# Order of data sums, bias joining and row transfers in a fused attention and non-local block

## The chip, the cores and the metric

One core of a Trainium2 chip runs the whole program. The metric is the device time in microseconds (us) of one execution; lower is better. The engines that matter are TensorE (PE in the profile: matrix products; PEld is its weight load), VectorE (DVE), ScalarE (ACT), GpSimd (POOL) and SyncE (SP), which issues the transfers (DMA).

## The reference

Eight images of 512 channels and 32 x 32 points, all in float32. Each goes through two layers:

```
# layer 0: attention, 8 heads of 64 channels
q, k, v = Wq x + bq,  Wk x + bk,  Wv x + bv          # 1x1 convolutions
out = softmax(q^T k / 8) v                            # per head, 1024 x 1024
x = x + Wp out + bp
# layer 1: non-local block, 256 inner channels
theta, phi, g = Wtheta x + bt,  Wphi x + bp2,  Wg x + bg
z = W ((theta phi^T / 1024) g) + bW + x
# then, per channel, over all images and points:
out = (z - mean(z)) / sqrt(var(z) + 1e-5) * gamma + beta
```

## The kernel before

The eight images are worked one after the other; the loop over `b` is unrolled, so the program is one long stream on each engine. An image passes through the stages attention (scores `ps`, weighted values `po`), q of the next image (`pq`), denominators (`den`), v of the next image (`pv`), k of the next image (`pk`), projection (`pp`), theta and phi (`ptp`), g (`pg`), theta times phi (`pf`), and the second layer's output (`pz`). Image 6 puts off its g and z, so that attention of image 7 follows its theta and phi at once.

**Seven products for eight.** Each 1x1 convolution is a product of 2 x 2 blocks done by a Strassen-Winograd scheme (`seven`, from L232): seven block products instead of eight, at the price of sums. The data sums are made by `data_sums` (L185): from the quarters 11, 12, 21, 22 of the data, t1 = 12 - 11, t2 = 22 - t1, t3 = 22 - 12, t4 = 21 - t2, each of 128 x 1024 on VectorE. The products use them in the order 11, t1, t2, 22, t3, 21, t4. In q, k and (images 1 to 6) the projection, two of the seven are split once more: `nested` (L217) runs small products between the large ones, on the inner sums of 21 and of t4 (`inner_sums`, four operations of 128 x 256 each). A product's result stands in a pair of PSUM banks; `first` takes it out with a bias, `add` adds it to another quarter. The next product that writes the bank waits until that is done. Four such pairs (`s0` to `s3`) rotate: the list `free` gives their order, and `next_bank` takes the next one.

**The order on an engine.** A scheduler orders each engine's instructions by priority, which is program order, and by when it reckons that their inputs are ready. Those given to `pe`, `dve` or `sp` (one function, `keep_in_program_order`) keep their order among themselves. On the chip each engine then takes its instructions in that fixed order. Blocks of 128 x 1024 (`block`) come from a ring of ten, shared by the exponentials, the data sums and other helpers; a new one waits for a block that is no longer read.

**Around the change.**
- End of attention: two steps before its end `near_end` makes the four data sums of the next image. The last exponential is summed into `acc` (L424). The last weighted values leave PSUM by a copy on ScalarE (L444) and a sum on VectorE (L445); the bank that they leave is one of the two that q's nested products take. Then come the inner sums of 21.
- `normalize` (L479) brings the reciprocals of the softmax denominators, one row per head and half, to all partitions: for each half h, group g of four units and head j of a pair, one transfer of 64 partitions x 2 rows of 2 KB into `r`. The transfers are issued before v; the four products `o * r` (L493) come after the fifth of v's seven products (`{4: normalize(d)}`). The data sums of o follow during k (`sums_of_o`).
- `bound_scores` (L375) multiplies the peaks of q and k, sums them over a head on TensorE (`bound`), compares (`gates`, L381) and multiplies q by the gate on GpSimd (L383), four operations of 128 x 1024. For images 1 to 7 it runs after the fifth product of the projection; for image 0 in v.
- `theta_phi` (L526): the result of the first product leaves PSUM by one sum on VectorE (L536), which frees the bank for the third product. Its data sums are all made before.
- `join_bias` (L173), once, ahead of the projection of image 0: Wp bv is added to bp, by 16 products with a single column, each of two passes, hence 32 matmuls in the profile.

Of the kernel before, what the change touches and what calls it, by code (L numbers as in the profile page):

```python
# [30 lines left out]
def unshifted(ctx: ExitStack, tc: tile.TileContext, a: dict, out: bass.AP):  # L31
# [31 lines left out]
    def pe(ins):  # L63
        tc.keep_in_program_order(ins)
# [8 lines left out]
    def next_bank(name):  # L73
        free.append(free.pop(0))
        return bank(free[-1], name)
# [96 lines left out]

    def join_bias(w):  # L173

        ps = next_bank("pbp")[:, 0, :CC]
        for oc in range(CC):
            m, mc = divmod(oc, CC // 2)
            for c in range(CC):
                k, kc = divmod(c, CC // 2)
                quarter = {(0, 0): w[:, 0], (0, 1): w[:, 1], (1, 0): corner["WpT"], (1, 1): w[:, 2]}[m, k]  # L180
                pe(nc.tensor.matmul(ps[:, oc:oc + 1], quarter[:, kc, mc * P:(mc + 1) * P], bv[:, c:c + 1],
                                    start=(c == 0), stop=(c == CC - 1), skip_group_check=True))
        nc.vector.tensor_tensor(bp, bp, ps, ALU.add)

    def data_sums(quarters, name, width=2, pin=lambda ins: None, midway=lambda: None):  # L185

        b11, b12, b21, b22 = quarters
        t = [block(f"t{i}_{name}")[:, :width, :] for i in range(4)]
        pin(nc.vector.tensor_tensor(t[0], b12, b11, ALU.subtract))  # L189
        pin(nc.vector.tensor_tensor(t[1], b22, t[0], ALU.subtract))  # L190
        midway()
        pin(nc.vector.tensor_tensor(t[2], b22, b12, ALU.subtract))
        pin(nc.vector.tensor_tensor(t[3], b21, t[1], ALU.subtract))
        return {"11": b11, "21": b21, "22": b22, "t1": t[0], "t2": t[1], "t3": t[2], "t4": t[3], "name": name}

    def inner_sums(data, which):
# [4 lines left out]
        nc.vector.tensor_tensor(t[:, 0], b12, b11, ALU.subtract)  # L201
        nc.vector.tensor_tensor(t[:, 1], b22, t[:, 0], ALU.subtract)
        nc.vector.tensor_tensor(t[:, 2], b22, b12, ALU.subtract)
        nc.vector.tensor_tensor(t[:, 3], b21, t[:, 1], ALU.subtract)
# [157 lines left out]
    def values(b, w, data, between=None):  # L362
        v = mats.tile([P, NB, C], F32, tag="v", name=f"v_{b}")

        def at(q):
            return v[:, (int(q[1]) - 1) * NB // 2:int(q[1]) * NB // 2, (int(q[0]) - 1) * C // 2:int(q[0]) * C // 2]

        def as_v(ps):
            return ps.rearrange("p h (i f) -> p (h i) f", f=C // 2)

        seven(f"pv_{b}", w, data, True, lambda q, ps: nc.scalar.copy(at(q), as_v(ps)),  # L371
              lambda q, ps: nc.vector.tensor_tensor(at(q), at(q), as_v(ps), ALU.add), between)
        return v

    def bound_scores(b, q, k, peak_q, peak_k):  # L375
# [14 lines left out]
    def attention(b, q, k, v, near_end, make_f=None):  # L390
# [16 lines left out]
        def scores(i):  # L407
            u, m = steps[i]
            p, h = units[u]
            ps = bank(tags[(0, 1, 3)[i] if i < 3 else (i + 1) % 2], f"ps_{b}_{u}_{m}")  # L410
            for j in range(2):
                r = slice(j * D, (j + 1) * D)
                for c in range(2):
                    keys = slice(m * P + c * P // 2, m * P + (c + 1) * P // 2)
                    pe(nc.tensor.matmul(ps[c * P // 2:(c + 1) * P // 2, j, :], k[r, p, keys],  # L415
                                        q[r, p, h * 512:(h + 1) * 512], start=True, stop=True, skip_group_check=True))
            e = block(f"e_{b}_{u}_{m}")
            nc.scalar.activation(e, ps, AF.Exp, scale=SCALE)  # L418
            es[u, m] = e
            if m == 1:  # L420
                accs[u] = w3.tile([P, 2, 512], F32, tag="acc", name=f"acc_{b}_{u}")
                nc.vector.tensor_tensor(accs[u], es[u, 0], e, ALU.add)  # L422
            elif m > 1:
                nc.vector.tensor_tensor(accs[u], accs[u], e, ALU.add)  # L424
            if m == NB - 1 and u == len(units) - 1 and make_f:
                near_end(lambda: spread(u, dve))
            elif m == NB - 1:
                spread(u)

        def weighted(i):  # L430
            u, m = steps[i]
            p, _ = units[u]
            if m == 0:
                sums[u] = bank(tags[2 + u % 2], f"po_{b}_{u}")
            ps, e = sums[u], es.pop((u, m))
            for r in range(2):
                keys = slice(r * P // 2, (r + 1) * P // 2)
                for j in range(2):
                    pe(nc.tensor.matmul(ps[j * D:(j + 1) * D, r, :], v[keys, m, (2 * p + j) * D:(2 * p + j + 1) * D],  # L439
                                        e[keys, j, :], start=(m == 0), stop=(m == NB - 1), skip_group_check=True))  # L440
            if m == NB - 1:
                if not o:
                    o["o"] = mats.tile([P, CC, N], F32, tag="o", name=f"o_{b}")
                nc.scalar.copy(part(u), ps[:, 0, :])  # L444
                nc.vector.tensor_tensor(part(u), part(u), ps[:, 1, :], ALU.add)  # L445

        def spread(u, pin=lambda ins: None):

# [30 lines left out]
        def normalize(d):  # L479

            r = foldp.tile([P, 8, 512], F32, tag="fold", name=f"r_{b}")
            for h in range(NH):
                for g in range(2):
                    for j in range(2):
                        rows_of = d[g].rearrange("(j p h s) n -> j h s p n", j=2, p=2, h=NH)[j, h, 0]
                        sp(nc.sync.dma_start(r[j * D:(j + 1) * D, 4 * g + h:4 * g + 4:2, :],
                                             rows_of.partition_broadcast(D)))

            def products():
                for h in range(NH):  # L490
                    for g in range(2):
                        at = o["o"][:, 2 * g:2 * g + 2, h * 512:(h + 1) * 512]
                        dve(nc.vector.tensor_tensor(at, at, r[:, 4 * g + h:4 * g + 4:2, :], ALU.mult))  # L493

            return products
# [27 lines left out]
              early=b == B - 1, inner="WpT" if 0 < b < B - 1 else None)  # L523


    def theta_phi(b, w, data):  # L526
        tp = mats.tile([P, NB, 2 * CI], F32, tag="o", name=f"tp_{b}")

        def at(q):
            return tp[:, (int(q[1]) - 1) * NB // 2:int(q[1]) * NB // 2, (int(q[0]) - 1) * CI:int(q[0]) * CI]  # L530

        def as_tp(ps):
            return ps.rearrange("p h (i f) -> p (h i) f", f=CI)

        seven(f"ptp_{b}", w, data, True,
              lambda q, ps: nc.vector.tensor_tensor(  # L536
                  at(q), as_tp(ps), tpb[:, int(q[0]) - 1].to_broadcast([P, NB // 2, CI]), ALU.add),
              lambda q, ps: nc.vector.tensor_tensor(at(q), at(q), as_tp(ps), ALU.add))
        return tp

    def make_f(b, tp, ps):
# [183 lines left out]
    for b in range(B):  # L725
# [5 lines left out]
        def near_end(midway=None):  # L731
            if last:
                nxt["data"] = data_sums(quarters_of(held["x"]), f"x1_{b - 1}_again", pin=dve, midway=midway)
            else:
                nxt["data"] = data_sums(quarters_of(nxt["x"]), f"x_{b + 1}")

        def held_f(ps):
            held["f"] = make_f(b - 1, held["tp"], ps)
# [288 lines left out]
```

## Time and profile before

| | |
|---|---|
| three timed executions | 2188.3, 2189.35, 2190.09 us |
| the profiled execution | 2190.26 us, span in the profile 2188.5 us |
| mean granted TensorE clock | 0.994 |
| one attention | 110 us |
| from one attention to the next, images 1 and 2 | 267.3 us |
| the same, image 3 | 272.1 us |

The profile is that of one execution. A timeline line reads: start, duration (both us), engine, source line, operation, output<-inputs, shape, count, and in brackets the idle time ahead of it with what ended it. A waits line reads: engine and line that waited, what for, us in total, times, longest. Matmuls of float32 run in two passes, so one product is two entries. A matmul's recorded end is modelled and overlaps the next one's start, so the distance between starts tells more than the duration.

### The profile page before, as it was taken

What the parts mean: (1) busy time and instruction counts of PE and PEld (TensorE: products, weight loads), DVE (VectorE), ACT (ScalarE), POOL (GpSimd) and SP (SyncE); (2) the same over time, 40 slices, a digit from 0 to 9 for tenths busy, and PEclk for the clock granted to TensorE, in tenths of its full rate; (3) what the DMA queues carried; (4) which work ended last, traced back from release to release, by engine and by line L of the source; (5) the groups of instructions that cost most, each with busy time, mean ns of one, the idle gap of its engine ahead of it and who ended that gap; (6) DMA issues with size and microseconds to landing.
All of it is one profiled execution on the core that took longest, in us unless ns stands there. A gap on an engine that the chain in (4) does not pass through costs nothing.

```text
span 2188.5 us, 29703 instructions
## 1 busy us (share of the span) xinstructions
PE 2149.1 (98%) x12478; PEld 1113.0 (51%) x12478; DVE 1434.5 (66%) x1612; ACT 741.6 (34%) x848; POOL 52.5 (2%) x36
## 2 busy tenths in 40 slices
PE   9999999999999999999999999999999999999996
PEld 4534664346633467335573356633666336643362
DVE  6477656777567764777647777477773677657736
ACT  1463103641046310463104631056212652056115
POOL 0000000000100001000010000100000000100000
PEclk9999999999999999999999999999999999999998
DMA  6312433114131231312413123231234114121559
GB/s 214 133 39 58 129 149 120 40 39 154 68 130 40 65 118 67 131 40 73 111 68 130 40 77 107 100 108 40 87 134 160 40 40 130 51 63 41 185 209 358
DMA packets 59405, 223.41 MB, mean 102 GB/s; under 512 B 9856, under 2 KB 16256, under 8 KB 53760
## 3 DMA queue, kind: packets, MB, share of 16 engines
q1 hardware_dynamic: 57776, 220.12, 31.1%
q8 instruction: 100, 1.64, 0.3%
q10 hardware_dynamic: 1488, 1.32, 0.2%
q14 instruction: 41, 0.34, 0.0%
HBM read 138.03 MB, written 49.81 MB: 86 GB/s over the span
## 4 chain that ended last, share of the span: by engine, by line
PE 87%; DVE 8%; DMA 2%; issue 1%; ACT 1%; SPq 0%; DVEq 0%
PE ps L415 20%; PE po L439 19%; PE ptp L268 7%; PE pp L268 7%; PE pv L268 7%; PE pk L268 6%; PE pq L268 5%; PE pg L268 4%; PE pf L546 3%; PE pz L268 2%; PE pk_in_s L231 2%; PE pq_in_s L231 2%; PE pp_in_s L231 2%; PE pz L656 2%; PE pwf L581 1%
## 5 line engine op out<-in xcount | busy, mean ns | idle before, releaser
L418 ACT ACTIVATE e<-ps 128x1024 f32<-128x1024 f32 x512 | 522.9, 1025 | 428.9 <-PE ps L415 424.0
L424 DVE TENSOR_TENSOR acc<-acc,e 128x1024 f32<-128x1024 f32 x384 | 470.1, 1224 | 129.4 <-ACT e L418 122.0
L439 PE MATMUL po<-e,v 64*64 64x512 f32 x4096 | 528.7, 589 | 0.7 <-ACT w_WgT L548 0.7
L415 PE MATMUL ps<-q,k 64*64 64x512 f32 x4096 | 529.1, 589 | 0.0
L439 PEld LDWEIGHTS po<-e,v 64*64 64x64 f32 x4096 | 156.5, 133 | 283.4 <-issue 275.4
L415 PEld LDWEIGHTS ps<-q,k 64*64 64x64 f32 x4096 | 155.6, 133 | 284.1 <-issue 274.7
L569 ACT ACTIVATE g<-pg,gb 128x512 f32<-128x512 f32 x31 | 21.3, 687 | 399.1 <-PE pg L268 396.2
L422 DVE TENSOR_TENSOR acc<-e,e 128x1024 f32<-128x1024 f32 x64 | 78.2, 1222 | 108.7 <-ACT e L418 73.4
L268 PE MATMUL ptp<-w_tp,t_x 128*128 128x256 f32 x512 | 116.3, 380 | 5.2 <-DVE tp L536 5.2
L268 PE MATMUL pv<-w_WvT,t_x 128*128 128x256 f32 x512 | 114.5, 379 | 0.0
L268 PEld LDWEIGHTS ptp<-w_tp,t_x 128*128 128x128 f32 x512 | 96.7, 190 | 20.9 <-DVE tp L536 8.1
L268 PEld LDWEIGHTS pv<-w_WvT,t_x 128*128 128x128 f32 x512 | 97.2, 190 | 13.2
L268 PE MATMUL pp<-t_o,w_WpT 128*128 128x512 f32 x208 | 101.0, 593 | 0.5 <-DVE t_o L189 0.5
L268 PE MATMUL pk<-t_x,w_WkT 128*128 128x512 f32 x200 | 100.1, 598 | 0.0
L268 PE MATMUL pq<-t_x,w_WqT 128*128 128x512 f32 x200 | 98.8, 593 | 0.3 <-DVE w_WqT L708 0.3
L371 ACT COPY v<-pv 128x1024 f32<-128x1024 f32 x32 | 32.4, 1012 | 191.2 <-PE pv L268 191.2
L383 POOL TENSOR_SCALAR q<-q,gates 128x1024 f32<-128x1024 f32 x32 | 52.2, 1649 | 1848.2 <-DVE gates L381 1848.2
L268 PE MATMUL ptp<-w_tp,x 128*128 128x256 f32 x384 | 87.4, 381 | 0.2 <-DVE x L290 0.2
L268 PE MATMUL pv<-w_WvT,x 128*128 128x256 f32 x384 | 87.5, 381 | 0.0
L268 PEld LDWEIGHTS pv<-w_WvT,x 128*128 128x128 f32 x384 | 72.4, 190 | 15.7 <-issue 5.9
L268 PEld LDWEIGHTS ptp<-w_tp,x 128*128 128x128 f32 x384 | 72.4, 190 | 11.0 <-DVE x L290 1.0
L466 DVE TENSOR_TENSOR fold<-fold 128x1024 f32<-128x1024 f32 x48 | 58.7, 1222 | 26.1 <-DMA fold<-acc 25.6
(186 smaller groups left out, 2216.0 us busy)
## 6 DMA issues: line engine op xcount, KB each, us to landing
fold<-acc SPq DMA_DIRECT2D x254, 128.0 KB, 2.3
r<-den_d SPq DMA_DIRECT2D x64, 256.0 KB, 7.0
x<-in_x_dram SPq DMA_DIRECT2D x31, 512.0 KB, 6.1
w_WqT<-kept_WqT SPq DMA_DIRECT2D x7, 2176.0 KB, 8.7
w_WkT<-kept_WkT SPq DMA_DIRECT2D x7, 2176.0 KB, 8.4
w_WpT<-kept_WpT SPq DMA_DIRECT2D x6, 2176.0 KB, 8.8
w_WvT<-kept_WvT SPq DMA_DIRECT2D x7, 1792.0 KB, 7.1
w_tp<-kept_tp SPq DMA_DIRECT2D x7, 1792.0 KB, 7.3
```

The source lines that it names most:

```text
L231: pe(nc.tensor.matmul(ps, a[wi], d[di], start=s not in begun, stop=True, skip_group_check=True))
L268: pe(nc.tensor.matmul(to_ps, lhsT(k), rhs(k), start=(s, at) not in begun, stop=(k == nk - 1), skip_group_check=True))
L371: seven(f"pv_{b}", w, data, True, lambda q, ps: nc.scalar.copy(at(q), as_v(ps)), lambda q, ps: nc.vector.tensor_tensor(at(q), at(q), as_v( ...
L383: nc.gpsimd.tensor_scalar(q[:, p, :], q[:, p, :], gate[:, p:p + 1], 1.0, ALU.mult, ALU.mult)
L415: pe(nc.tensor.matmul(ps[c * P // 2:(c + 1) * P // 2, j, :], k[r, p, keys], q[r, p, h * 512:(h + 1) * 512], start=True, stop=True, skip_gr ...
L418: nc.scalar.activation(e, ps, AF.Exp, scale=SCALE)
L422: nc.vector.tensor_tensor(accs[u], es[u, 0], e, ALU.add)
L424: nc.vector.tensor_tensor(accs[u], accs[u], e, ALU.add)
L439: pe(nc.tensor.matmul(ps[j * D:(j + 1) * D, r, :], v[keys, m, (2 * p + j) * D:(2 * p + j + 1) * D], e[keys, j, :], start=(m == 0), stop=(m ...
L466: return [lambda to=to, l=l, r=r: pin(nc.vector.tensor_tensor(to, l, r, ALU.add)) for to, l, r in ((t[:, 0], t[:, 0], t[:, 1]), (t[:, 2], ...
L546: pe(nc.tensor.matmul(ps[:, c, :], tp[:, i, c * P:(c + 1) * P], tp[:, i, CI:], start=(i == 0), stop=(i == NB - 1)))
L656: pe(nc.tensor.matmul(ps[:, h - h0, :], wf[:, d, oc * P:(oc + 1) * P], g[d][:, h * 512:(h + 1) * 512], start=(d == 0), stop=(d == IC - 1), ...
```

## The change

Five things:

1. `data_sums` can make some of the four sums, and `more_sums` the rest later. For the next image's q, t1 and t2 stay near the end of attention; t3 and t4 follow after the inner sums of 21. All of these from the last `acc` and last `o` sum on are held in program order, the inner sums of t4 too. For theta/phi, t1 and t2 stay ahead; t3 and t4 come after the sum that takes out the first product.
2. `bound_scores` moves from the projection to theta/phi, after its fourth product.
3. `normalize` brings the rows by four transfers of four rows each instead of eight of two; the products `o * r` come after v's sixth product instead of its fifth.
4. The sums into v are held in program order.
5. `join_bias` multiplies the blocks of Wp by bv and sums them over the four chunks on GpSimd (eight scalings and six sums of 128 x 256), into a block of the ring; TensorE then needs four products with a column of ones.

```diff
     def join_bias(w):
+        t = block("wp_bv")
+        half = C // 2
+        for m, quarters in enumerate(((w[:, 0], w[:, 1]), (corner["WpT"], w[:, 2]))):
+            to, one = (t[:, i, m * half:(m + 1) * half] for i in range(2))
+            for c in range(CC):
+                nc.gpsimd.tensor_scalar(one if c else to, quarters[c // 2][:, c % 2, :], bv[:, c:c + 1], 1.0,
+                                        ALU.mult, ALU.mult)
+                if c:
+                    nc.gpsimd.tensor_tensor(to, to, one, ALU.add)
         ps = next_bank("pbp")[:, 0, :CC]
         for oc in range(CC):
-            m, mc = divmod(oc, CC // 2)
-            for c in range(CC):
...
+            pe(nc.tensor.matmul(ps[:, oc:oc + 1], t[:, 0, oc * P:(oc + 1) * P], ones, start=True, stop=True,
+                                skip_group_check=True))
         nc.vector.tensor_tensor(bp, bp, ps, ALU.add)
...
+    def data_sums(quarters, name, which=(1, 2, 3, 4), **how):
+        data = dict(zip(("11", "12", "21", "22"), quarters), name=name)
+        more_sums(data, which, **how)
+        return data
+
+    def more_sums(data, which, pin=lambda ins: None, midway=lambda: None):
+        for i in which:
+            l, r = {1: ("12", "11"), 2: ("22", "t1"), 3: ("22", "12"), 4: ("21", "t2")}[i]
+            if i == 3:
+                midway()
+            data[f"t{i}"] = block(f"t{i}_{data['name']}")
+            pin(nc.vector.tensor_tensor(data[f"t{i}"], data[l], data[r], ALU.subtract))
...
         seven(f"pv_{b}", w, data, True, lambda q, ps: nc.scalar.copy(at(q), as_v(ps)),
-              lambda q, ps: nc.vector.tensor_tensor(at(q), at(q), as_v(ps), ALU.add), between)
+              lambda q, ps: dve(nc.vector.tensor_tensor(at(q), at(q), as_v(ps), ALU.add)), between)
...
-                nc.vector.tensor_tensor(accs[u], accs[u], e, ALU.add)
+                ins = nc.vector.tensor_tensor(accs[u], accs[u], e, ALU.add)
+                if i == len(steps) - 1 and not make_f:
+                    dve(ins)
...
-                nc.vector.tensor_tensor(part(u), part(u), ps[:, 1, :], ALU.add)
+                ins = nc.vector.tensor_tensor(part(u), part(u), ps[:, 1, :], ALU.add)
+                if i == len(steps) - 1 and not make_f:
+                    dve(ins)
...
-            for h in range(NH):
-                for g in range(2):
-                    for j in range(2):
-                        rows_of = d[g].rearrange("(j p h s) n -> j h s p n", j=2, p=2, h=NH)[j, h, 0]
-                        sp(nc.sync.dma_start(r[j * D:(j + 1) * D, 4 * g + h:4 * g + 4:2, :],
-                                             rows_of.partition_broadcast(D)))
+            for g in range(2):
+                for j in range(2):
+                    rows_of = d[g].rearrange("(j i s) n -> j s i n", j=2, i=4)[j, 0]
+                    sp(nc.sync.dma_start(r[j * D:(j + 1) * D, 4 * g:4 * g + 4, :], rows_of.partition_broadcast(D)))
...
-    def theta_phi(b, w, data):
+    def theta_phi(b, w, data, between):
...
+        def first(q, ps):
+            ins = nc.vector.tensor_tensor(at(q), as_tp(ps), tpb[:, int(q[0]) - 1].to_broadcast([P, NB // 2, CI]),
+                                          ALU.add)
+            if q == "11":
+                dve(ins)
+
+        seven(f"ptp_{b}", w, data, True, first,
+              lambda q, ps: nc.vector.tensor_tensor(at(q), at(q), as_tp(ps), ALU.add),
+              {0: lambda: more_sums(data, (3, 4), pin=dve), **between})
...
-                nxt["data"] = data_sums(quarters_of(nxt["x"]), f"x_{b + 1}")
+                nxt["data"] = data_sums(quarters_of(nxt["x"]), f"x_{b + 1}", (1, 2))
...
-            inner_sums(nxt["data"], "21")
+            inner_sums(nxt["data"], "21", dve)
+            more_sums(nxt["data"], (3, 4), dve)
             q, peak_q = heads_of(b + 1, "q", weights("WqT"), bq, nxt["data"], dve, inner="WqT",
-                                 between={1: lambda: inner_sums(nxt["data"], "t4")}, fills=last_fold)
+                                 between={1: lambda: inner_sums(nxt["data"], "t4", dve)}, fills=last_fold)
             load_w(nc.sync)
             d = [denominators(g, next_bank(f"den_{b}_{g}")[:, 0, :]) for g in range(2)]
-            v = values(b + 1, weights("WvT"), nxt["data"], {4: normalize(d)})
+            v = values(b + 1, weights("WvT"), nxt["data"], {5: normalize(d)})
...
-            between = {4: lambda: bound_scores(b + 1, q, k, peak_q, peak_k)}
...
-        data = data_sums(quarters_of(xt), f"x1_{b}")
+        data = data_sums(quarters_of(xt), f"x1_{b}", (1, 2))
...
-        tp = theta_phi(b, weights("tp"), data)
+        tp = theta_phi(b, weights("tp"), data, {} if last else {3: lambda: bound_scores(b + 1, q, k, peak_q, peak_k)})
```

More of the change, by code (lines that the diff above doesn't have):

```diff
@@ L175, in join_bias @@
         ps = next_bank("pbp")[:, 0, :CC]
         for oc in range(CC):
-            m, mc = divmod(oc, CC // 2)
-            for c in range(CC):
[L179 to L182, printed above, removed]
@@ L183, in join_bias @@
-        nc.vector.tensor_tensor(bp, bp, ps, ALU.add)
[L185 to L194, printed above, removed]
@@ L196, in inner_sums @@
-    def inner_sums(data, which):
+            pe(nc.tensor.matmul(ps[:, oc:oc + 1], t[:, 0, oc * P:(oc + 1) * P], ones, start=True, stop=True,
+                                skip_group_check=True))
+        nc.vector.tensor_tensor(bp, bp, ps, ALU.add)
+    def data_sums(quarters, name, which=(1, 2, 3, 4), **how):
[9 more added lines that the diff above has]
+            pin(nc.vector.tensor_tensor(data[f"t{i}"], data[l], data[r], ALU.subtract))
@@ L198, in inner_sums @@
+    def inner_sums(data, which, pin=lambda ins: None):
         d, name = data[which], f"{which}_{data['name']}"
@@ L200, in inner_sums @@
         t = block(f"i_{name}").rearrange("p a (b n) -> p (a b) n", b=2)
[L201 to L204, printed above, removed]
+        pin(nc.vector.tensor_tensor(t[:, 0], b12, b11, ALU.subtract))
+        pin(nc.vector.tensor_tensor(t[:, 1], b22, t[:, 0], ALU.subtract))
+        pin(nc.vector.tensor_tensor(t[:, 2], b22, b12, ALU.subtract))
+        pin(nc.vector.tensor_tensor(t[:, 3], b21, t[:, 1], ALU.subtract))
         data[f"inner {which}"] = {"11": b11, "21": b21, "22": b22, **{f"t{i + 1}": t[:, i] for i in range(4)}}
@@ L533, in as_tp @@
             return ps.rearrange("p h (i f) -> p (h i) f", f=CI)
[L535 to L538, printed above, removed]
+        def first(q, ps):
[6 more added lines that the diff above has]
+              {0: lambda: more_sums(data, (3, 4), pin=dve), **between})
         return tp
```

## The prediction

> **What bounds the kernel now.** I read the busy shares first, then TensorE's own waits, then the timeline of each place those waits name. The busy shares say that TensorE is the bound:
>
> ```profile
> PE 2149.1 (98%) x12478; PEld 1113.0 (51%) x12478; DVE 1434.5 (66%) x1612; ACT 741.6 (34%) x848; POOL 52.5 (2%) x36
> ```
>
> So a gain can come only from gaps in TensorE's stream or from matmuls left out. Its waits, the longest groups:
>
> ```profile
> PE ptp L268 <- DVE tp L536: 5.2, 7, 0.8
> PE pq_in_s L231 <- DVE o L445: 5.0, 7, 0.7
> PE pk_in_s L231 <- DVE k L290: 3.2, 2, 2.8
> ```
>
> Two come once in each of the images 0 to 6; the third comes in two images only. Busy time runs on past a matmul's start, so I price a wait by starts. The wait in q, image 0, on TensorE and VectorE:
>
> ```profile
> 193.69 1.02 PE L268 MATMUL pq<-t_x,w_WqT 128*128 128x512 f32 x2
> 195.42 0.70 PE L231 MATMUL pq_in_s<-i_x,w_WqT 128*128 128x256 f32 x2 [0.71 <-DVE o L445]
> 195.96 1.02 PE L268 MATMUL pq<-t_x,w_WqT 128*128 128x512 f32 x2
> 194.69 0.68 DVE L445 TENSOR_TENSOR o<-o,po 128x512 f32<-128x512 f32 x1
> ```
>
> The pair at 193.69 takes 0.86 (the step before, 192.40 to 193.26), so the next was due at 194.55 and came 0.87 late; it then took 0.54 to the next start where its kind takes 0.43. **Price 0.97 us.** VectorE's sum frees the bank that the nested product writes; it stood behind four sums of data and eight inner ones. The wait in theta/phi, image 1:
>
> ```profile
> 569.98 3.72 PE L268 MATMUL ptp<-w_tp,t_x 128*128 128x256 f32 x16 [0.76 <-DVE tp L536]
> 566.74 2.06 DVE L193 TENSOR_TENSOR t_x<-x,t_x 128x1024 f32<-128x1024 f32 x1
> 568.72 2.34 DVE L536 TENSOR_TENSOR tp<-ptp,tpb 128x1024 f32<-128x1024 f32 x2
> ```
>
> The product before began at 565.61 and takes 3.45, so 569.06 was due: 0.92 late, 0.10 more in its own run (573.54 follows after 3.56). **Price 1.02 us**, 0.93 in image 0. Third, join_bias in image 0:
>
> ```profile
> 266.78 0.99 PE L181 MATMUL pbp<-bvc,w_WpT 128*128 128x1 f32 x4
> 267.64 6.15 PE L268 MATMUL pp<-o,w_WpT 128*128 128x512 f32 x8
> 267.60:273.60 6.00, 6.00 (x9) 2.58 (x10) 2.41 (x3) 0.00 (x0) 0.00 (x0) 0.58 0.01 3
> ```
>
> The last is a stretch with its granted clock, 0.58. The 32 passes of one column run from 263.26 to 267.64, and the eight passes of the projection after them take 5.98 where such eight take 3.43 elsewhere. Fourth, the k stage, which normalize feeds, in images 1 and 3:
>
> ```profile
> 517.28 1.23 DVE L493 TENSOR_TENSOR o<-o,r 128x1024 f32<-128x1024 f32 x1 [0.85 <-DMA r<-den_d]
> 520.82 0.41 DVE L290 TENSOR_TENSOR k<-k,pk_in_s 128x256 f32<-128x256 f32 x1
> 522.38 0.59 PE L231 MATMUL pk_in_s<-i_x,w_WkT 128*128 128x256 f32 x2
> ...
> 1051.33 1.23 DVE L493 TENSOR_TENSOR o<-o,r 128x1024 f32<-128x1024 f32 x1 [5.55 <-DMA r<-den_d]
> 1059.53 0.41 DVE L290 TENSOR_TENSOR k<-k,pk_in_s 128x256 f32<-128x256 f32 x1
> 1059.99 0.70 PE L231 MATMUL pk_in_s<-i_x,w_WkT 128*128 128x256 f32 x2 [2.83 <-DVE k L290]
> ```
>
> In image 1 the first sum into k ends at 521.23 and the third nested product, which overwrites its bank, comes at 522.38: slack 1.1. In image 3 a late row transfer holds VectorE. Two images are 534.6 apart (q starts at 465.0 and 999.6), so that sum was 4.1 late; the image took 272.1 from attention to attention, the others 267.3: 4.8 lost.
>
> **The Trainium skill.** "TensorE: Matmul & The Clock Gate", What's actually happening: after an idle window of about 3.4 us the clock is halved, in free-running windows. The trace agrees: 0.5 granted for 6.8 us from 265.8 on, after the tiny matmuls, and for 3.4 us after the stop at 1057. "GPSIMD Engine Reference", 3.1 Elementwise: a two-input sum of 2048 elements takes 4497 ns; no run here shows one. The same page, 8 Key points: GpSimd shares its SBUF interfaces with VectorE instructions of two SBUF inputs. It agrees: 2.06 for the sum above instead of 1.22 while GpSimd scales q, and GpSimd's scaling takes 1.12 in the median, 2.98 at most. "DMA: Bandwidth & Descriptors", Anatomy of one DMA: some 2 us fixed and the rest by bytes; the store of the denominators lands 2.0 after its issue, the 256 KB rows 7.0 in the median, as they queue.
>
> **The change part by part.**
> *q.* No work is added: t3, t4 move from before to after the last o sum and the inner sums of 21, and the order is pinned. New order for image 0: last acc to about 189.7; o sum (needs ScalarE's copy, 189.00 + 0.59) to 190.4; four inner sums at 0.34 to 191.7; t3, t4 at 1.14 to 194.0. The bank is wanted at 194.55: met by 4 us. Behind t3, t4 wait the sums into q: the first is ready at 193.85, loses 0.1, and its bank is wanted 2 us later. The four inner sums of t4 (1.35), pinned between fourth and fifth nested sum, delay the fifth by 0.5 with 2 to spare. Gain 7 x 0.97 = **6.8**.
> *theta/phi.* The sum tp of "11" now goes ahead of t3, t4: ready at 565.8, done at 567.0, wanted at 569.06. t2 ends at 565.6 as now, t3 at 568.1 (wanted at the fifth product, 576), t4 at 569.3. Gain 6 x 1.02 + 0.93 = **7.1**. Image 7 has no such wait.
> *Scaling of q.* Four GpSimd operations (7.2) go from 564.8 to some 578 on; what they slow is sums of tp, with 2.2 idle between them. In image 6, where attention follows at once, the gates can come at about 1906, the scaling ends by 1914, and the first quarter is wanted at 1915: hidden. The bank rotation shifts by one; each bank that the next product takes was read 2 us or more earlier. Cost 0, at worst 1 in image 6.
> *Bias.* Eight passes instead of 32: 4.38 / 32 = 0.137 each, 1.1 in all. Saved 3.3, and with a gap of 1 us no halved clock, 2.55 more: **5.8**. GpSimd's work is 8 scalings and 6 sums of 256 elements. Scalings: 0.28 (a quarter of 1.12) to 0.75 (of 2.98), I take 0.35; sums: 0.42 (VectorE's own) to 1.1 (twice the estimate of 4497 / 8 = 0.56 from the page above), I take 0.65. Together 4.8 to 12.6, 6.7 taken. It starts once the weights are there (247 at most; VectorE first uses the last quarter at 247.0) and a ring block is free; the block for the corner of Wg, next in program order, is loaded at 253.7. So it ends between 252 and 266, taken 260.4; TensorE wants it at 263.3. Hidden, with 3 us lost at the far end.
> *Rows.* SP issues four transfers for eight, the same 2 MB in the same 2 KB rows. Eight take 6.8 us to issue and 14.6 from the first issue to the last landing in image 1 (502.63 to 517.26): they are bound by moving bytes, so I leave the last landing where it is (at best 2 earlier). But the second product now needs the second half of the rows, hence the last transfer, and the products stand one product of v later. Image 1: first product at 513.3, second from 517.3, fourth ends at 520.7 instead of 518.5, and the first t sum of o comes after it instead of before: 521.8. The first sum into k then ends at 522.2 if one t sum precedes it, at 523.3 if two do; wanted at 522.38. So 0 to 1.3 lost an image. Image 0, whose transfers land 1 later and which loses 0.66 already, 1 to 4. I take 0.3 in each of 1, 2, 4, 5, 6 and 1.5 in image 0; image 3 keeps its loss. The pinned sums of v no longer stand behind a late row. Cost **3**.
>
> Sum on the profiled span: 2188.5 - 6.8 - 7.1 - 5.8 + 3 = 2171.8. The profiled execution took 2190.26 with all around it, the three timed ones 2189.35 in the median (2188.30 to 2190.09); the same 16.7 off the median gives **2172.6**.
>
> **Rivals.**
> A, VectorE late in k: the upper ends above (1.3 x 5 + 4 + 1.5 for image 3) make 12 of the 3, so 2181.7. For: two t sums may stand ahead; against: they are not pinned, and k comes first in program order.
> B, GpSimd late: a ring block that comes only at k's end (261.5) plus 6.7 stops TensorE for 5 us, and the clock halves again: the 5.8 goes, 2178.4.
> C, rows faster: the last landing 2 earlier removes image 0's 0.66, the cost of 3, and image 3's 4.8 if that transfer was late by chance: 2189.35 - 19.7 - 5.4 = 2164.3. The three times lie too close together to show such a chance.
> D, the other side: all second products wait so long that VectorE is over 4 us late in k everywhere, as in image 3 now: 7 x 4.8 = 33.6 against 19.7, so 2203. It decides above 2.8 us lost an image, which is 3.9 late. For: the mechanism is in the trace; against: it needs 2.5 more than my reckoning of image 1.
> That a pinned order is not what I work out belongs to A and D.
>
> **Numbers.** Likeliest 0.62; A 0.14, B 0.10, C 0.07, D 0.07. The range 2164 to 2182 takes in all but D and the far ends. Within 0.2% (4.4 us) is about what a measurement can't tell from no change: faster 0.89, same 0.04, slower 0.07.
>
> **What would show it.** TensorE's waits on L445's o sum and L536's tp sum gone; passes before the first projection 1 us and the clock at 1.00 there; GpSimd's bias work ended before TensorE asks; the second product waiting for rows and the waits of pk_in_s on k under 1 us an image. Wrong if a new wait of over 1 us an image appears at pk_in_s, or the clock falls at the bias.

## The result, and the profile after

| | before | changed |
|---|---|---|
| median of six timed executions | 2188.55 us | 2181.67 us |
| lowest to highest | 2186.46 to 2190.09 | 2179.27 to 2183.88 |
| ratio, with 95% interval | | 0.997 (0.9957 to 0.9983) |
| span in the profile | 2188.5 us | 2180.1 us |

The changed kernel is faster by 6.9 us; 16.7 had been forecast. The time lies just inside the range of the forecast (2164 to 2182), but that is luck: two errors, shown below, partly cancel. The two traces show at once that this is not a gain that came out small everywhere. In the table, an image runs from the first score matmul of its attention to that of the next, the last one to the end of the span; the numbers are distances between TensorE's starts in the timelines.

| image | 0 | 1 | 2 | 3 | 4 | 5 | 6 | 7 to the end |
|---|---|---|---|---|---|---|---|---|
| before | 276.1 | 267.3 | 267.3 | 272.1 | 267.3 | 254.9 | 232.5 | 272.2 |
| changed | 268.7 | 265.5 | 265.4 | 268.3 | 265.3 | 252.9 | 230.8 | 284.6 |
| difference | -7.4 | -1.8 | -1.9 | -3.8 | -2.0 | -2.0 | -1.7 | **+12.4** |

Images 0 to 6 gained 20.7 us, 4 more than forecast for the whole. Image 7 gave 12.4 back, and the prediction has no loss there at all.

TensorE's busy share is what it was. First the changed kernel's page, then the longest groups of TensorE's waits (us in total, times, longest):

```profile
PE 2142.0 (98%) x12454; PEld 1109.4 (51%) x12454; DVE 1423.3 (65%) x1612; ACT 741.5 (34%) x848; POOL 45.1 (2%) x50
```

```profile
PE pp L276 <- issue: 5.2, 1, 5.2
PE pk_in_s L239 <- DVE k L298: 3.0, 2, 2.2
PE pp L276 <- DVE o L503: 2.6, 1, 2.6
PE ptp L276 <- DVE t_x L202: 2.4, 1, 2.4
```

The two sevenfold waits, on the o sum and on the sum tp, are gone. In their place stand three waits that come once each, all in image 7: two ahead of products of the projection and one in theta/phi. (The second line above, the waits in k, belongs to images 0 and 3; before, it was 3.2.) What the forecast said of images 0 to 6 is seen in the timelines of the same places. Image 0 in q, where the step after 193.54 now comes 0.86 later and on time, and the VectorE order behind it:

```profile
193.54 1.02 PE L276 MATMUL pq<-t_x,w_WqT 128*128 128x512 f32 x2
194.40 0.59 PE L239 MATMUL pq_in_s<-i_x,w_WqT 128*128 128x256 f32 x2
...
189.58 0.68 DVE L455 TENSOR_TENSOR o<-o,po 128x512 f32<-128x512 f32 x1
191.65 1.22 DVE L202 TENSOR_TENSOR t_x<-x 128x1024 f32<-128x1024 f32 x1
```

Image 1 in theta/phi (one run of 32 passes, with no gap before the third product), and image 0's bias, the last fence being the stretch ahead of the projection's first product, with the clock in the third column from the end:

```profile
556.97 7.07 PE L276 MATMUL ptp<-w_tp,t_x 128*128 128x256 f32 x32
557.17 1.23 DVE L546 TENSOR_TENSOR tp<-ptp,tpb 128x1024 f32<-128x1024 f32 x1
```

```profile
262.52 0.72 POOL L183 TENSOR_TENSOR wp_bv<-wp_bv 128x256 f32<-128x256 f32 x1
263.13 0.95 PE L186 MATMUL pbp<-ones,wp_bv 128*128 128x1 f32 x8
263.94 3.68 PE L276 MATMUL pp<-o,w_WpT 128*128 128x512 f32 x8
```

```profile
261.80:263.90 2.10, 2.10 (x12) 1.34 (x10) 1.51 (x2) 0.29 (x1) 1.36 (x3) 1.00 0.80 338
```

Eight passes take 0.8 us, and the first product of the projection its full-clock 3.5 (263.94 to 267.45). Now image 7, TensorE and then VectorE:

```profile
2032.46 3.60 PE L671 MATMUL pz<-g,wf 128*128 128x512 f32 x8
2041.24 5.88 PE L276 MATMUL pp<-o,w_WpT 128*128 128x512 f32 x8 [5.18 <-issue]
2049.76 3.70 PE L276 MATMUL pp<-o,w_WpT 128*128 128x512 f32 x8 [2.63 <-DVE o L503]
2086.89 5.27 PE L276 MATMUL ptp<-w_tp,t_x 128*128 128x256 f32 x16 [2.45 <-DVE t_x L202]
...
2039.91 1.23 DVE L503 TENSOR_TENSOR o<-o,r 128x1024 f32<-128x1024 f32 x1 [9.00 <-DMA r<-den_d]
2047.16 1.41 DVE L530 SCALAR_TENSOR_TENSOR x<-pp,bp,x 128x512 f32<-128x512 f32 x2 [6.02 <-PE pp L276]
2048.49 3.49 DVE L503 TENSOR_TENSOR o<-o,r 128x1024 f32<-128x1024 f32 x3
2084.48 1.22 DVE L552 TENSOR_TENSOR tp<-tp,ptp 128x1024 f32<-128x1024 f32 x1 [2.23 <-PE ptp L276]
2085.61 1.22 DVE L202 TENSOR_TENSOR t_x<-x 128x1024 f32<-128x1024 f32 x1
```

TensorE stands still ahead of the projection, because the first product o * r waited for its rows until 2039.9 (the profile names no releaser there, "issue", but that product ends 0.1 us before TensorE starts). The clock is halved around it (0.5 granted for 6.8 us from 2038.9). TensorE waits again for the second product o * r, whose rows landed at 2046.3, but which stands on VectorE behind two bias sums that wait for TensorE. And in theta/phi it waits for t3, which VectorE made only behind three further sums of tp. The lead over the kernel before, read at the start of each stage of image 7: g 20.9 us, z 20.7, projection 16.8, theta/phi 12.6, g 8.4, end 8.4. So 3.9 are lost ahead of the projection, 4.1 inside it and 4.3 in theta/phi.

### The profile page after: what moved, and what is told of

The parts are those of the page before. It is cut to its first block, busy times and chain, and to the rows that moved or that the text cites. A ratio compares the mean times of both kernels' runs of the same rounds, so it can differ in the third digit from the quotient of the medians.

```text
span 2180.1 us, 29638 instructions
## 1 busy us (share of the span) xinstructions
PE 2142.0 (98%) x12454; PEld 1109.4 (51%) x12454; DVE 1423.3 (65%) x1612; ACT 741.5 (34%) x848; POOL 45.1 (2%) x50
## 4 chain that ended last, share of the span: by engine, by line
PE 93%; DMA 2%; DVE 2%; issue 1%; ACT 1%; SPq 0%; DVEq 0%
PE ps L423 20%; PE po L449 20%; PE ptp L276 9%; PE pp L276 7%; PE pv L276 7%; PE pq L276 6%; PE pk L276 6%; PE pg L276 4%; PE pf L561 3%; PE pz L276 2%; PE pk_in_s L239 2%; PE pq_in_s L239 2%; PE pp_in_s L239 2%; PE pz L671 2%; DMA r<-den_d 1%; PE pwf L596 1%
## 5 line engine op out<-in xcount | busy, mean ns | idle before, releaser
L380 DVE TENSOR_TENSOR v<-v,pv 128x1024 f32<-128x1024 f32 x24 | 29.3, 1222 | 79.9 <-PE pv L276 79.9
L276 PEld LDWEIGHTS pv<-w_WvT,x 128*128 128x128 f32 x384 | 72.4, 190 | 15.7 <-issue 5.9
L276 PEld LDWEIGHTS ptp<-w_tp,x 128*128 128x128 f32 x384 | 73.0, 190 | 13.3 <-issue 3.6
L276 PE MATMUL pp<-o,w_WpT 128*128 128x512 f32 x144 | 70.1, 611 | 7.8 <-issue 5.2
```

The costliest lines, as they stand in the source:

```text
L276: pe(nc.tensor.matmul(to_ps, lhsT(k), rhs(k), start=(s, at) not in begun, stop=(k == nk - 1), skip_group_check=True))
L380: lambda q, ps: dve(nc.vector.tensor_tensor(at(q), at(q), as_v(ps), ALU.add)), between)
```

## The experiments

**Theory G**: the gain of images 0 to 6 is as worked out; the loss is image 7's alone, from two parts of the change that only that image feels: rows that come in larger groups where nothing hides them, and t3, t4 that come late. **Rival L**: image 7 is held by transfers that don't move up, so any lead is lost there. The other rivals are named in the expectations. Times are medians, ratios are to the kernel before on the same chip. The runs used four chips; the kernel before has medians of 2187.76 to 2188.32 us on them, so a difference between runs of different chips is uncertain by some half a us from that alone.

### Image 7's rows by eight transfers again (e1)

```diff
-            for g in range(2):
-                for j in range(2):
-                    rows_of = d[g].rearrange("(j i s) n -> j s i n", j=2, i=4)[j, 0]
...
+            if make_f:       # image 7 alone
+                for h, g in [(h, g) for h in range(NH) for g in range(2)]:
+                    for j in range(2):
+                        rows_of = d[g].rearrange("(j p h s) n -> j h s p n", j=2, p=2, h=NH)[j, h, 0]
```

> The changed kernel with the rows of image 7 by eight transfers again; images 0 to 6 keep four. Theory G (grouping): in image 7 nothing hides the rows, and with four transfers the first product waits for half of the bytes (9.2 us after the first issue) instead of a quarter (5.5). Undone, TensorE's wait ahead of the projection falls from 5.2 to about 1.3 us, the halved clock after it goes, and 8 of the 12.4 us lost in image 7 come back: 2173.6 us. Rival L (loads): image 7 is held by transfers that don't move up when the images before it end 21 us earlier, so that any lead is lost there: no gain, 2181.7 us. Rival Q (queue): fewer transfers let the reloads behind them on SyncE start earlier and contend with the rows; then the last row lands as early as in the kernel before (14.6 us after the first issue) rather than 15.7, with 2 to 3 us gained.

2172.82 us, ratio 0.9933 (0.9912 to 0.9955): 8.9 us of the loss came back. TensorE's wait ahead of the projection is 1.3 us:

```profile
2037.68 7.11 PE L276 MATMUL pp<-o,w_WpT 128*128 128x512 f32 x16 [1.29 <-issue]
2079.20 3.72 PE L276 MATMUL ptp<-w_tp,t_x 128*128 128x256 f32 x16 [2.45 <-DVE t_x L202]
```

Theory G holds. Rival Q fails: in image 7 the last row lands 14.4 us after the first issue here, as in the kernel before (14.6), but the gain is far more than the 1.3 us that this is earlier than in the changed kernel (15.7). The wait in theta/phi stands as before, but no halved clock follows it here: the product takes its usual 3.6 us, where the changed kernel's took 5.1.

### Image 7's four data sums ahead again (e2), and both (e3)

```diff
-        data = data_sums(quarters_of(xt), f"x1_{b}", (1, 2))
+        data = data_sums(quarters_of(xt), f"x1_{b}", (1, 2, 3, 4) if last else (1, 2))
...
-              {0: lambda: more_sums(data, (3, 4), pin=dve), **between})
+              {**({} if b == B - 1 else {0: lambda: more_sums(data, (3, 4), pin=dve)}), **between})
```

> The changed kernel with all four data sums of image 7's theta/phi ahead of the stage, as in the kernel before; nothing else is undone. Theory G with B (blocks): t3 stood behind three sums of tp on VectorE, TensorE waited 2.45 us for it and ran 3.4 us at half clock, 4.3 us in all: 2177.4 us, and that wait gone from the trace. Rival L: no gain, since the wait only moves to a later place in image 7: 2181.7 us.

> Both undone in image 7 alone. Theory G with B: the two add, as they lie one after the other on TensorE: 2169.3 us, 19 us under the kernel before, and the time from the start of g in image 7 to the end as in the kernel before. Rival L: 2180 to 2182 us.

The sums alone: 2177.06 us, ratio 0.9957 (0.9944 to 0.9969), 4.6 less, and the wait for t_x is gone. Both: 2170.04 us, 0.9923 (0.9902 to 0.9944). From attention of image 7 to the end of the span it is 272.8 us, against 272.2 in the kernel before. The two don't quite add (8.9 + 4.6 = 13.5, together 11.6). The traces show one reason: what either wait costs depends on whether the clock is halved after it, and that changed between runs with other things held (1.5 us in e1's theta/phi, above). e2's own profile has another such stretch, of 3.4 us, in the projection, so its image 7 is only 2.9 us shorter than the changed kernel's. The lead of 21 us now reaches the end, so rival L falls. Kernel e3 is the base of what follows, if not said otherwise.

### Why t3 was late: the ring or the order (e4)

```diff
         if last:
-            reload_chunks(B - LATE)
...
         tp = theta_phi(b, weights("tp"), data, ...)
+        if last:
+            reload_chunks(B - LATE)
```

> The changed kernel, where image 7 asks for the four blocks of the reloaded image 5 after theta/phi instead of ahead of it; t3 and t4 stay behind the first sum of tp. Theory B (blocks): t3 came late because those four took the ring's blocks first; now t3 and t4 follow the first sum of tp, the wait of 2.45 us goes, 2177.4 us or up to 2 more where the reload comes late. Rival P (order): t3 is late because it is held in program order with the late sums; then its place and the wait stay, 2181.7 us.

2178.56 us, ratio 0.9963 (0.9949 to 0.9976). t3 and t4 now follow the first sum of tp, though they are held in order as in the changed kernel:

```profile
2074.51 1.23 DVE L546 TENSOR_TENSOR tp<-ptp,tpb 128x1024 f32<-128x1024 f32 x1 [0.87 <-PE ptp L276]
2075.65 1.21 DVE L202 TENSOR_TENSOR t_x<-x 128x1024 f32<-128x1024 f32 x1
2076.78 1.22 DVE L202 TENSOR_TENSOR t_x<-x,t_x 128x1024 f32<-128x1024 f32 x1
```

Theory B holds. In image 7 the reload of image 5 takes four of the ten blocks; once t3 and t4 are asked for after it, they get theirs later, and the scheduler fills VectorE's order with what is ready. The loss is in that order, fixed ahead of the run: in the changed kernel's trace the last signal that t3 waits for came by 2075.4, 10 us before t3 began, and VectorE idled three times in between.

### The parts in images 0 to 6, one undone at a time (e5 to e8, e11)

The edits, from the base: `join_bias` with its 32 passes (e5); the order around q (e6: `data_sums(..., f"x_{b + 1}")` whole near the end of attention, no `dve` on the last acc, the last o sum and the inner sums); all sums of theta/phi ahead of it, the first tp sum not held (e7); `bound_scores` after the projection's fifth product (e8); e7 and e8 at once (e11).

> From here on the base is the changed kernel with image 7 mended (rows by eight and four sums ahead there), 2170.0 us. Here its bias is joined on TensorE again, by 32 passes. Theory G: 5.8 us more, 2175.8: 3.3 of them in the passes, 2.5 from the halved clock after them (0.5 granted for 6.8 us near 265). Rival K: the clock falls only by where the free-running window happens to lie, so no halved clock this time and 3.3 more alone, 2173.3 us.

> The base with the order around q as in the kernel before: four data sums ahead of attention's end, last acc, last o sum and inner sums not held. Theory G: TensorE waits 0.87 us in each of seven images for the last o sum, 0.97 with the slow start after it: 6.8 more, 2176.8 us. Rival N: the wait is part of a time that the next stages make up (VectorE gets its sums done earlier), so under 3 more.

> The base with all four data sums ahead of theta/phi's first sum again in every image; the scaling of q stays late. Theory S (slowing): the wait of 0.9 us in theta/phi came to 0.84 from GpSimd slowing the fourth sum (2.06 instead of 1.22 us); with the scaling gone from there the sum of the first product ends at about the time it is wanted, so 0.1 to 0.2 an image: 1 more, 2171 us. Theory G as predicted (order): the order is what removes the wait, 7.1 more, 2177.1 us.

> The base with the scaling of q back in the projection, so that GpSimd works as theta/phi begins; the order of the sums stays changed. Theory S and theory G agree that no wait comes back, since the sum of the first product goes ahead of the slowed ones: within 1 us of 2170.0. Rival X: GpSimd slows that sum or t2 too, and 0.3 or more an image comes back, 2172 us or more.

> The base with both the sums of theta/phi and the scaling of q as in the kernel before. The two alone cost 1.5 and nothing. Theory S (slowing and order are two ways to remove the same wait): undone together the wait of 0.9 us comes back in each of seven images, 7.1 more, 2177.1 us. Rival M: the wait has another cause, so that the two add up to 1 or 2 us: 2171 us.

| undone | time | against 2170.04 | ratio to before | image 4 |
|---|---|---|---|---|
| nothing (e3) | 2170.04 | | 0.9923 (0.9902 to 0.9944) | 265.30 |
| bias (e5) | 2175.65 | +5.6 | 0.9945 (0.9929 to 0.9962) | 265.30 |
| order in q (e6) | 2176.23 | +6.2 | 0.9946 (0.9929 to 0.9962) | 266.28 |
| sums of theta/phi (e7) | 2171.53 | +1.5 | 0.9923 (0.9907 to 0.9940) | 265.65 |
| scaling of q (e8) | 2169.13 | -0.9 | 0.9915 (0.9899 to 0.9932) | 265.30 |
| both of theta/phi (e11) | 2176.74 | +6.7 | 0.9949 (0.9932 to 0.9966) | 266.33 |

Image 4 is shown because its rows are on time in every run. The order in q is worth 0.98 us an image; rival N falls. The bias is as predicted in the time. In e5's profile, though, image 0 is only 3.6 us longer than in e3's: the clock was halved for 3.4 us there, not 6.8 as in the kernel before. So K is right in that the length differs from run to run, and G in that the halved clock comes. The agreement of 5.6 with 5.8 rests on four executions, two near 2174.5 and two near 2177, and may be luck in part.

Theta/phi is where the reason was incomplete. The wait is worth 1.03 us an image (266.33 - 265.30), as predicted, but **either** change removes most of it. e7 and e11 differ only in where GpSimd works; the lines are VectorE's t4 and the tp sum behind it, e7 first:

```profile
558.29 1.22 DVE L202 TENSOR_TENSOR t_x<-x,t_x 128x1024 f32<-128x1024 f32 x1
559.43 2.46 DVE L553 TENSOR_TENSOR tp<-ptp,tpb 128x1024 f32<-128x1024 f32 x2
```

```profile
559.20 2.06 DVE L202 TENSOR_TENSOR t_x<-x,t_x 128x1024 f32<-128x1024 f32 x1
561.17 2.34 DVE L553 TENSOR_TENSOR tp<-ptp,tpb 128x1024 f32<-128x1024 f32 x2
```

A sum that GpSimd slows from 1.22 to 2.06 us was most of the wait, 0.68 of 1.03 (266.33 - 265.65). With the order changed, the place of the scaling is worth nothing that these times show (e8).

### What it is about the rows (e9, e10, e12, e13)

e9: image 7's eight transfers in the order `for g in range(2) for h in range(NH)`. e10: eight transfers in every image. e12: the kernel before with four transfers in image 7 alone. e13, from e2: the projection's bias sums in image 7 held with `dve`.

> The base (changed kernel with image 7 mended, 2170.0 us); in image 7 the eight transfers in the order of groups (both halves of the first group, then both of the second) instead of halves. Theory G (what counts is how many bytes are queued ahead of the rows that a product wants): the first product as before, 5.5 us after the first issue; the second wants the sixth transfer, some 11.2, instead of the fourth, 8.5. TensorE then waits about 2 us ahead of the second product of the projection: 2172 us. Rival C (the number and size of transfers): eight are eight, 2170.0 us.

> The base with eight row transfers in all images. Theory G: in images 1, 2, 4, 5, 6 nothing changes, as the waits there are hidden; in images 0 and 3, whose last row lands 16 to 17 us after the first issue, only the last product follows the last landing instead of three, so VectorE is up to 2.3 us earlier in k and most of the 2.6 us of waits and 1 to 2 of halved clock go: 2166 to 2168 us. Rival C: four transfers cost nothing in images 0 to 6, 2170.0 us, the waits in k as they were.

> The kernel before with four row transfers in image 7 alone. Theory G: the loss doesn't depend on how early image 7 begins: 8 us more than before, 2196 us, with a wait of some 5 us ahead of the projection. Rival L (a lead is what is lost): without a lead nothing is lost, within 2 us of before.

> The kernel of e2 (four row transfers in image 7, four sums ahead there; 2177.1 us), with the bias sums that take out the projection's products in image 7 held in program order, so that they stand behind the four products of o and rows. Theory O (order): part of the loss is the bias sum that VectorE had ahead of the second product, itself waiting for TensorE at half clock; the second product now begins when its rows land, 1 to 2 us earlier, and TensorE's second wait (2.6) shrinks by as much: 2175 to 2176 us. Theory R (rows alone): the second product begins no earlier, since the rows are what it waits for: 2177.1 us; later than that if the bias sums now hold the banks.

e12: 2197.94 us, ratio 1.0045 (1.0029 to 1.0062). Alone, on the kernel before, the four transfers of image 7 cost 10.2 us by the times and lengthen image 7 by 10.4 in the traces, with no lead to lose: rival L is ruled out a second time, and this one edit makes the kernel slower.

e9: 2172.30 us, 0.9932 (0.9915 to 0.9948), as theory G has it: the number of transfers is the same, only what is queued first differs, and TensorE waits 2.63 us ahead of the projection's second product. In e1 (halves first) it doesn't. The sixth transfer, which that product o * r needs, landed at 2040.73, and the product began at 2041.01, so nearly all of this wait is the rows' and not VectorE's order.

```profile
2035.97 3.67 PE L276 MATMUL pp<-o,w_WpT 128*128 128x512 f32 x8 [1.36 <-issue]
2042.28 3.70 PE L276 MATMUL pp<-o,w_WpT 128*128 128x512 f32 x8 [2.63 <-DVE o L510]
```

e13: 2175.61 us, 0.9943 (0.9926 to 0.9959), 1.45 less than e2. With the bias sum behind the products, the second product begins when the rows land instead of behind a sum that waits for TensorE; TensorE's wait for it falls from 2.6 to 0.3, and 1.1 comes back as a wait on the bias sums. First e2, then e13:

```profile
2044.97 1.41 DVE L530 SCALAR_TENSOR_TENSOR x<-pp,bp,x 128x512 f32<-128x512 f32 x2 [6.45 <-PE pp L276]
2046.30 3.48 DVE L503 TENSOR_TENSOR o<-o,r 128x1024 f32<-128x1024 f32 x3
```

```profile
2044.59 3.50 DVE L503 TENSOR_TENSOR o<-o,r 128x1024 f32<-128x1024 f32 x3 [5.36 <-DMA r<-den_d]
2052.66 1.40 DVE L531 SCALAR_TENSOR_TENSOR x<-pp,bp,x 128x512 f32<-128x512 f32 x2
```

So both O and R hold in part: of some 7 us that the four transfers cost on this base (e2 2177.06 against e3 2170.04), about 1.5 are VectorE's order and the rest the later rows with the halved clock. The two aren't cleanly apart: e2's trace has a second halved stretch, of 3.4 us, behind the second wait, and e13's has none there.

e10: 2168.38 us, 0.9914 (0.9897 to 0.9930), 1.7 less than the base. That is within the range of theory G, though with executions from 2166.3 to 2169.6 it is not far from the scatter. The trace has image 0's wait in k gone and image 3's at 1.6 us instead of 2.1, with no halved clock there. That is not shown to come of the eight transfers: e2, e4, e8 and e9, with four, have no wait in image 0 either, and e15 below, with eight, waits 3.7 us in image 3.

### The later place of the products, and the best mix (e14, e15)

e14, from e10: `{4: normalize(d)}` again. e15: e10 with the scaling of q back in the projection.

> The kernel of e10 (eight row transfers everywhere, 2168.4 us) with the products of o and rows after v's fifth product again, as in the kernel before; the sums into v stay held in order. Theory E (early): with eight transfers the first rows are there by then, so the fourth product still follows the last landing and nothing changes: 2168.4 us. Rival H (held): the third sum into v stands behind products that wait for late rows, which holds a bank that k wants; in images 0 and 3, 1 to 3 us more, 2170 us or more.

> The kernel of e10 (eight row transfers everywhere) with the scaling of q back in the projection as in e8. Theory S: the scaling costs nothing in either place, so 2168.4 us as e10; the two changes touch different stages and add: 2167.5 us if e8's 0.9 was real.

e14: 2172.32 us, 0.9924 (0.9908 to 0.9941), 3.9 more than e10. e15: 2168.90 us, 0.9912 (0.9895 to 0.9928).

Rival H holds in its mechanism: what TensorE waits for in e14's image 3 is the held sum into v. Its size is not settled. e14's image 3 takes 272.8 us in the profile and e10's 267.2, but the rows came late in one and not in the other: the fourth of eight transfers landed 14.1 us after the first issue in e14 and 10.3 in e10. In e15, which keeps e10's order, it landed at 13.6, and image 3 takes 270.8, with a wait for a sum into k. First e14, then e15:

```profile
1045.41 1.22 PE L239 MATMUL pk_in_s<-x,w_WkT 128*128 128x256 f32 x2 [4.29 <-DVE v L380]
```

```profile
1046.84 1.22 PE L239 MATMUL pk_in_s<-i_x,w_WkT 128*128 128x256 f32 x2 [3.73 <-DVE k L298]
```

With rows late in both, the place of the products makes 2.0 us in image 3, most of it a halved clock of 6.8 us instead of 3.4. How the rows came in the timed executions is not on record.

e15 is no better than e10: e8's gain of 0.9 does not come back, and is taken for scatter. e10 and e15 are the fastest kernels of the study, some 19 us under the kernel before and 13 under the changed one; between the two the runs don't decide.

## Why the prediction was right or wrong

**q: right.** Predicted 0.97 an image and 6.8; the trace has 0.98, the undoing 6.2. VectorE's order came out within 0.2 us of the one worked out (o sum at 189.58, t3 at 191.65).

**Theta/phi: right in size for images 0 to 6, half of the reason missing.** Predicted 7.1, measured 6.7. The prediction read the 2.06 us of t4 and named GpSimd as its cause, but credited the whole gain to the order and gave the moved scaling cost 0 and gain 0. It should have asked what the stage would be with either edit alone. e7 answers 0.35 us an image lost.

**Theta/phi in image 7: the first step that failed.** "Image 7 has no such wait" is true, and the step stopped there. Before, t3's product came there without a wait:

```profile
2096.91 3.62 PE L268 MATMUL ptp<-w_tp,t_x 128*128 128x256 f32 x16
```

That image gets the new order too, with nothing to gain from it, and its ring is the fullest of all: four blocks for a reload are asked for between t2 and t3. The prediction described the ring as a limit for the bias block and didn't count it here. Cost 4.3 in the trace, 4.6 by e2.

**Rows: the step that failed most.** It worked out the landing for image 1, found that the second product now needs the last transfer, and priced that where v and k hide it. `normalize` is called in image 7 as well, with the products at once and the projection behind them. The code says so, and so does the trace before, where VectorE waits for rows and TensorE behind it:

```profile
2058.01 7.11 PE L268 MATMUL pp<-o,w_WpT 128*128 128x512 f32 x16 [1.25 <-issue]
2056.68 1.23 DVE L493 TENSOR_TENSOR o<-o,r 128x1024 f32<-128x1024 f32 x1 [5.07 <-DMA r<-den_d]
2059.76 1.23 DVE L493 TENSOR_TENSOR o<-o,r 128x1024 f32<-128x1024 f32 x1 [1.85 <-DMA r<-den_d]
```

By the same rule that the prediction used, the first product wants half of the bytes instead of a quarter: 9.2 us after the first issue against 5.5 in the two traces, 3.9 on TensorE ahead of the projection. A halved clock of 6.8 us goes with it in all five profiles that have four transfers in image 7, and in none with eight. The second product o * r came later still, 2.2 us behind the last landing, for the bias sums ahead of it on VectorE; e13 puts that part at about 1.5. Cost 8.0 in the trace, 8.9 by e1.

**Rows in images 0 to 6: overpriced.** Predicted a cost of 3. The last landing stayed about where it was, as said (image 1: 15.2 us after the first issue, 14.6 before), but VectorE took the first sum into k ahead of all t sums of o:

```profile
509.45 3.50 DVE L503 TENSOR_TENSOR o<-o,r 128x1024 f32<-128x1024 f32 x3 [3.42 <-DMA r<-den_d]
512.87 0.41 DVE L298 TENSOR_TENSOR k<-k,pk_in_s 128x256 f32<-128x256 f32 x1
513.20 1.22 DVE L202 TENSOR_TENSOR t_o<-o 128x1024 f32<-128x1024 f32 x1
```

so the first sum into k was in time. With four transfers (e3) and with eight (e10) images 1, 2 and 4 take the same 265.3 us, 5 the same 252.85 and 6 the same 230.49, so four transfers cost nothing there, where 0.3 each was taken. Image 0 waits 0.85 in k instead of 0.40, but between 0 and 1.0 in other runs with four transfers. (A slip without effect: of the sixteen stores of the denominators, said to land 2.0 us after issue, eight do; the others take 2.9 to 4.0.)

**Image 3: a gain that was not priced, in part luck.** The prediction left its loss as it was; it gained 3.8 us, of which q and theta/phi explain 2.0. It waits 2.2 in k instead of 2.8 and has no halved clock. Its last row landed 17.1 us after the first issue instead of 18.5, and the sums into v no longer stand behind a late row. The prediction saw the second and gave it no value; e14 shows that such a wait for v comes back when this is undone. But e1 and e3, which work image 3 in the same way, have a halved clock there and take 269.8 and 269.3 us instead of 268.3.

**Bias: right in the time.** Predicted 5.8, measured 5.6 by e5 (3.6 in its profile, above). GpSimd began at 253.56, as reckoned from the ring (253.7), but took 9.7 us instead of 6.7: the scalings 0.47 where 0.35 was taken, the first two 1.34 each, the sums 0.72 for 0.65. It ended at 263.24 with TensorE asking at 263.13 for a part already done. The margin of 3 us was used up whole. The prediction also says that the trace agrees with an idle window of some 3.4 us. Only the lengths of the halved stretches do (3.4 and 6.8): the 32 passes ran for 4.4 us without a stop, and the stop near 1057 was 2.83 us.

**The rivals.** None was the right one. A's figure, 2181.7, is what was measured, but by chance: it puts the loss in k, where almost nothing was lost. D has the right mechanism, a product that waits for the last transfer, in the wrong images. C allowed that image 3's late rows were a chance. They land last in every profile, but how late varies (the fourth of eight transfers at 10.3 us in e10, at 13.3 to 14.1 in the four others), so C was right in part. Beside e1 to e4, two of thirteen executions of the kernel before took 2181.3 and 2181.4 us; there is no trace of them, and what they were spared stays open.

**The sum.** The expected gain for images 0 to 6 was 16.7 and the measured one 20.7. Of the 4 more, 3 are the cost of the rows that did not come and 1.8 are image 3's, less small losses. The errors in images 0 to 6 and in image 7 have opposite signs, and without the 4 more the time would have left the range.

## What to carry to other kernels

A helper that a change touches is to be priced once for each place that calls it, the last trip of an unrolled loop above all: what hides a transfer in seven images may not exist in the eighth. Where a consumer starts on the first part of a split transfer, merging transfers costs the time of the bytes now queued ahead of that part: here 3.8 us, while the last landing moved by 1.1. And when one change removes a wait by two edits, take one away at a time: here one of the two was enough.

## What the runs showed of the hardware that had not been expected

- Passes of a single column did not keep TensorE's clock up: around 32 of them in 4.4 us it was halved in all three profiles that have them, for 6.8 us in one and for 3.4 in the two others (e5 and e12). With eight passes in 0.8 us it was halved at that place in none of fourteen profiles.
- Short stops were met by a halved clock in some runs and not in others. A stop of 2.45 us in theta/phi went with 3.4 us of it in the changed kernel and with none in e1, with the same work on both sides. In image 3's k, waits of 1.9 to 2.8 us were followed by 3.4 us of it in seven profiles and by none in five.
- The rows of image 3 land last in every profile, 16.7 to 18.7 us after the first issue, and those of images 1, 2, 4 and 5 at 13.3 to 15.6. In the kernel before, their packets of 2 KB take longer (189 ns in the mean, 111 to 142 in images 1, 2, 4 and 5), single ones up to 3.6 us. No other transfer that the trace shows explains it, and no run here tells the cause: it stays open.
